# Head softmax of a two-layer hybrid: denominators over four heads instead of eight, summed by two adding transfers in a row, normalization in place

## The chip, the cores and the metric

The kernel runs on one core of a Trainium2 chip. The metric is the device time of one execution in microseconds (us); the median over runs is what is compared.

## The reference

The reference is a chain of two layers over 2 x 1024 tokens of width 128: latent attention, a spiking FFN, a state-space block, the spiking FFN again, linear attention, an FFN of eight experts, attention with 16 heads of width 8, and the experts once more. The change lies in the attention with 16 heads, whose softmax runs over the heads (axis 1), not over the keys:

```python
qkv = x @ w_qkv + b_qkv
qkv = qkv.reshape(b, n, 3, N_HEADS, HEAD_DIM)
qkv = jnp.transpose(qkv, (2, 0, 3, 1, 4))
q, k, v = (qkv[0], qkv[1], qkv[2])
dp = jnp.einsum('bhqd,bhkd->bhqk', q, k) * SCALE
attn = jax.nn.softmax(dp, axis=1)
w_avg = jnp.einsum('bhqk,bhkd->bhqd', attn, v)
```

So for each pair of a query and a key, 16 exponentials are summed and each is divided by that sum. All data are float32.

## The kernel before

All work of this stage stands in `heads_and_experts` (L928 to L1187), in one order written out by hand (`tc.manual_schedule`). It works on 128 blocks: two batches, eight tiles of 128 queries, eight tiles of 128 keys. In a block the partitions are keys and the free dimension is 16 heads x 128 queries.

A block goes through these functions: `products` (TensorE, L1025: 16 heads of scores into the one PSUM buffer `h_s`); `maxima` (VectorE, L1039: maximum over the heads); `exponentials` (VectorE subtracts the maximum into `h_e`, L1047; ScalarE takes two exponentials of eight heads each, L1050, in place); `lower` (SP issues a transfer that copies heads 0 to 7 into `h_e2`, L1056); `upper` (POOL issues an adding transfer that adds heads 8 to 15 to it, L1060); `denominators` (TensorE adds the remaining eight slices with eight multiplications by the identity into `h_pd`, L1065; a float32 multiplication stands in the profile as two records); `inverse` (VectorE reciprocal, L1070); `normalize` (POOL multiplies all 2048 columns by the reciprocal into `h_a`, two buffers, L1075); `weigh` (TensorE, values times weights, into `h_po`, L1081).

The loop at L1137 makes one step for each i from -1 to 131 and staggers the blocks. In step i TensorE's order is: `products` of block i+1, outputs of the experts (L905), the projection when a row of blocks is done (L1145), products of the experts (L879), `denominators` of block i-1, `weigh` of block i-3. VectorE's order is: `inverse` of block i-2, two multiplications for the experts (L894), `maxima` of block i+1, an addition to the residual (L914), the subtraction of block i+1. ScalarE's is: the gates of the experts (L886), the exponentials of block i+1. POOL's is: `normalize` of block i-2, then the issue of `upper` of block i. SP issues only the copy. Every engine keeps to its order, so that an instruction that waits holds up all that is behind it. `h_pd` is one PSUM buffer shared by `denominators` and the experts' outputs; `h_e` has four buffers, `h_e2` three.

Beside this run the experts of 256-token chunks (`ExpertStream`, L837): two units in each step, 32 units in a chunk. What prepares them, and the projections of the second batch (`preparation(1)`), stands in a list `side` (L1091), whose entries are begun when enough rows of blocks are `finished` and at most eight units are left; `aside(place)` puts one of their steps at its place. A step in which a preparing TensorE step is taken has no expert products (L1147). Units that are left at the end are worked off by the loop at L1179. After it `experts_ffn(g, w, [3])` works on the last 512 tokens alone.

Of the kernel before, what the change touches and what calls it, by code (L numbers as in the profile page):

```python
# [9 lines left out]
F32 = mybir.dt.float32  # L10
BF16 = mybir.dt.bfloat16
AF = mybir.ActivationFunctionType
ALU = mybir.AluOpType
# [6 lines left out]
P = 128  # L20
# [907 lines left out]
def heads_and_experts(g, w, first, second):  # L928

    nc, tc = g.nc, g.tc  # L930
    J, K, HD, H = 4, 4, 8, 16
    scale = HD**-0.5
    with ExitStack() as es:
# [3 lines left out]
        work = pool("h_work", 2)  # L937
# [20 lines left out]
        ex = ExpertStream(g, w, ework, ps_e)  # L958
# [61 lines left out]
        def spread(b):  # L1020
            v = vs[b].rearrange("p t (j k d) -> p (t j) k d", j=J, k=K)
            for k in range(K):
                nc.scalar.copy(vz[:, :, k, k, :], v[:, :, k, :])

        def products(b, qb, kb):  # L1025

            s = ps_s.tile([P, J, 512], F32, name="h_s")
            for j in range(J):
                quad = slice(32 * j, 32 * j + 32)
                nc.tensor.matmul(  # L1030
                    s[:, j, :].rearrange("p (k q) -> p k q", k=K),
                    kTs[b][quad, bass.ts(kb, P)],
                    qzs[b][quad, :, bass.ts(qb, P)],
                    start=True,
                    stop=True,
                )
            return s.rearrange("p j (k q) -> p (j k) q", k=K)

        def maxima(heads):  # L1039
            m = work.tile([P, P], F32, name="h_m")  # L1040
            nc.vector.tensor_reduce(m, heads.rearrange("p h q -> p q h"), AX.X, ALU.max)  # L1041
            return m

        def exponentials(heads, m):

            e = work.tile([P, H, P], F32, name="h_e", bufs=4)
            nc.vector.tensor_sub(e, heads, m.unsqueeze(1).to_broadcast([P, H, P]))  # L1047
            for half in range(2):
                eh = e[:, 8 * half : 8 * half + 8, :]
                nc.scalar.activation(eh, eh, AF.Exp, scale=scale)  # L1050
            return e


        def lower(e):
            e2 = work.tile([P, 8, P], F32, name="h_e2", bufs=3)
            nc.sync.dma_start(out=e2, in_=e[:, 0:8, :])  # L1056
            return e2

        def upper(e2, e):
            nc.gpsimd.dma_start(out=e2, in_=e[:, 8:16, :], accum_op=ALU.add)  # L1060

        def denominators(e2):
            pd = ps_d.tile([P, 4, D], F32, name="h_pd")[:, 0, :]
            for k in range(8):
                nc.tensor.matmul(pd, g.ident, e2[:, k, :], start=(k == 0), stop=(k == 7))  # L1065
            return pd

        def inverse(pd):
            r = work.tile([P, P], F32, name="h_r")
            nc.vector.reciprocal(r, pd)  # L1070
            return r

        def normalize(e, r):
            a = work.tile([P, H, P], F32, name="h_a")
            nc.gpsimd.tensor_mul(a, e, r.unsqueeze(1).to_broadcast([P, H, P]))  # L1075
            return a

        def weigh(kb, a, po):
            for k in range(K):
                for j in range(J):  # L1080
                    nc.tensor.matmul(  # L1081
                        po[32 * j : 32 * j + 32, :],
                        vz[:, kb * J + j, k].rearrange("p a d -> p (a d)"),
                        a[:, 4 * j + k, :],
                        start=(kb == 0 and k == 0),
                        stop=(kb == TPB - 1 and k == K - 1),
                    )

        side = [(2 * c + 2, ex.opening(c)) for c in second]  # L1091
        side.insert(2, (0, preparation(1)))
        side = [(0, ex.opening(c)) for c in first[1:]] + side
        finished, current, head = 0, None, None

        def aside(place):

            nonlocal current, head
            while True:
                if head is None:  # L1100
                    if current is None:
                        if not side or side[0][0] > finished or len(ex.units) > 8:
                            return False
                        current = side.pop(0)[1]
# [15 lines left out]
        blocks = [(b, qb, kb) for b in range(B) for qb in range(TPB) for kb in range(TPB)]  # L1120
        n = len(blocks)
        with tc.manual_schedule(engines=ALL):
            for _, step in ex.opening(first[0]):
                step()
            for place, step in preparation(0):
                step()
                if place != "act":
                    po = ps_d.tile([P, 4, D], F32, name="h_pd")
                    ex.outputs(po)
                    ex.add()  # L1130
                    ex.products()
                    ex.gates()
                    ex.multiply()
            spread(0)
            e_, e2_, d_, a_ = {}, {}, {}, {}
            oT = po = None
            for i in range(-1, n + 4):  # L1137
                if i + 1 < n:
                    heads = products(*blocks[i + 1])
                r = inverse(d_.pop(i - 2)) if 0 <= i - 2 < n else None  # L1140
                if ex.ready or oT is not None:
                    pd = ps_d.tile([P, 4, D], F32, name="h_pd")
                    ex.outputs(pd)
# [12 lines left out]
                aside("act")  # L1156
                ex.gates()
                if i + 1 < n:
                    e_[i + 1] = exponentials(heads, m)
                    e2_[i + 1] = lower(e_[i + 1])  # L1160
                aside("dve")
                if 0 <= i - 1 < n:
                    d_[i - 1] = denominators(e2_.pop(i - 1))
                if r is not None:
                    a_[i - 2] = normalize(e_.pop(i - 2), r)
                if 0 <= i < n:
                    upper(e2_[i], e_[i])
                aside("pool")
                if 0 <= i - 3 < n:
                    b, qb, kb = blocks[i - 3]  # L1170
                    if kb == 0:
                        po = ps_o.tile([P, P], F32, name="h_po")
                    weigh(kb, a_.pop(i - 3), po)
                    if kb == TPB - 1:
                        oT = work.tile([P, P], F32, name="h_oT")
                        nc.scalar.copy(oT, po)
                        if qb == TPB - 1 and b + 1 < B:
                            spread(b + 1)
            while ex.units or ex.fresh or ex.gated or ex.ready or side or current:  # L1179
                while any([aside(place) for place in ("dve", "act", "pool", "pe")]):  # L1180
                    pass
                po = ps_d.tile([P, 4, D], F32, name="h_pd")
                ex.outputs(po)
                ex.add()
                ex.products()
                ex.gates()
                ex.multiply()  # L1187
# [91 lines left out]
def kernel(ctx: ExitStack, tc: tile.TileContext, d: dict, out: bass.AP):  # L1279
# [108 lines left out]
```

## Time and profile before

| what | us |
|---|---|
| median of 3 runs (2315.94 to 2333.15) | 2323.1 |
| profiled execution, its own time | 2328.53 |
| its span, first to last instruction | 2326.8 |
| first to last `maxima` (L1041), 127 steps | 1307.8 to 2190.2 |
| last projection of the heads (L1145) | 2217.1 |
| first instruction of the last experts on TensorE (L96) | 2237.37 |

The profile is of one execution, 5.4 us above the median of the runs. From 1307.8 to 2190.2 it shows TensorE busy for 818.39 us, VectorE for 791.66, ScalarE for 612.54, POOL for 689.90, and a mean DMA share of 0.59. "Idle before" in its rows is the time for which an engine stood still just before an instruction, with the one that released it. The records of matmuls overlap, so times between starts are better than durations for TensorE.

### The profile page before, as it was taken

Reading aid. Unit: us, or ns where it says so; the run is one execution under the profiler, and the core shown is the slowest. Engines: PE = TensorE matmul, PEld = TensorE weight load, DVE = VectorE, ACT = ScalarE, POOL = GpSimd, SP = SyncE. Lnnn points to the kernel's source line nnn. Section 1 sums busy time; section 2 is a strip of 40 time slices with the busy share of each in tenths; the row PEclk is TensorE's granted clock in tenths of the full one; section 3 lists DMA queues with packets and bytes.
Section 4 is the critical chain, followed back from the end, with each engine's and each line's share of the span. In section 5 each row is a group of like instructions: output and inputs, shape, how many; then the busy total and the mean of one; then the engine's idle time right before and its main releaser. Section 6 shows DMA issues by size and latency. Waiting matters only on the chain. (4 is left out here: it accounts for less than half of the span.)

```text
span 2326.8 us, 36810 instructions
## 1 busy us (share of the span) xinstructions
PE 2015.9 (87%) x15152; PEld 1184.5 (51%) x15152; DVE 1629.0 (70%) x1988; ACT 1183.5 (51%) x1486; POOL 854.9 (37%) x460
## 2 busy tenths in 40 slices
PE   7779988887987748789698799999977999999999
PEld 4323344323334313235345577677755777777754
DVE  5851047788974659993423699899978999999732
ACT  1014521353643458764322576777735777777632
POOL 0001100033320000000102277878788787877700
PEclk9789997878998879899799899999989999999999
DMA  3000000076732067640000266566556665665500
GB/s 86 1 1 1 2 1 1 18 190 152 185 93 89 4 159 184 162 106 0 1 1 0 64 153 157 145 152 157 146 150 152 157 155 155 153 162 146 137 5 5
DMA packets 72647, 220.19 MB, mean 95 GB/s; under 512 B 9056, under 2 KB 19744, under 8 KB 72352
## 3 DMA queue, kind: packets, MB, share of 16 engines
q1 hardware_dynamic: 53584, 149.40, 21.5%
q0 software_dynamic: 18432, 67.12, 15.3%
q8 instruction: 119, 1.95, 0.3%
q10 hardware_dynamic: 464, 1.33, 0.3%
q14 instruction: 48, 0.39, 0.1%
HBM read 78.35 MB, written 5.24 MB: 36 GB/s over the span
## 5 line engine op out<-in xcount | busy, mean ns | idle before, releaser
L1075 POOL TENSOR_TENSOR h_a<-h_e,h_r 128x2048 f32<-128x2048 f32 x128 | 581.4, 4542 | 130.4 <-PE h_po L1081 93.9
L1041 DVE TENSOR_REDUCE h_m<-h_s 128x128 f32<-128x2048 f32 x128 | 293.2, 2291 | 73.2 <-PE h_s L1030 73.1
L1065 PE MATMUL h_pd<-h_e,ident 128*128 128x128 f32 x2048 | 267.4, 285 | 43.4 <-DMA h_e<-h_e 29.6
L1050 ACT ACTIVATE h_e<-h_e 128x1024 f32<-128x1024 f32 x256 | 256.5, 1049 | 89.6 <-DVE h_e L1047 71.4
L1047 DVE TENSOR_TENSOR h_e<-h_s,h_m 128x2048 f32<-128x2048 f32 x128 | 292.6, 2286 | 3.4 <-DVE h_m L1041 1.7
L1065 PEld LDWEIGHTS h_pd<-h_e,ident 128*128 128x128 f32 x2048 | 244.6, 196 | 87.3 <-DVE x_res L914 41.5
L304 POOL TENSOR_SCALAR_AFFINE_SELECT a_pT<-a_pT 128x256 f32<-128x256 f32 x128 | 97.2, 775 | 431.4 <-ACT a_pT L301 430.5
L301 ACT ACTIVATE a_pT<-a_st 128x1024 f32<-128x1024 f32 (+1 forms) x192 | 145.1, 808 | 139.1 <-PE a_st L291 137.0
L886 ACT ACT_TABLE_LOAD x105 | 134.7, 1283 | 150.5 <-PE e_pgu L879 150.3
L806 DVE TENSOR_TENSOR e_h<-e_sg,e_pu 128x512 f32<-128x512 f32 x128 | 87.0, 686 | 176.5 <-PE e_pu L802 151.2
L243 DVE TENSOR_REDUCE a_nm<-a_s 128x2 f32<-128x1024 f32 (+7 forms) x144 | 168.4, 1218 | 48.5 <-PE a_s L234 24.2
L804 ACT ACTIVATE e_sg<-e_pg 128x512 f32<-128x512 f32 x128 | 76.0, 596 | 192.5 <-PE e_pg L801 192.3
L825 PE MATMUL e_po<-e_h,Wd 128*128 128x512 f32 x256 | 139.4, 630 | 39.4 <-DVE e_h L806 39.3
L225 PE MATMUL a_s<-a_latT,a_qT 32*128 32x512 f32 (+3 forms) x768 | 128.7, 650 | 49.4 <-DVE a_nm L243 47.6
L905 PEld LDWEIGHTS h_pd<-Wd,e_h 128*128 128x128 f32 x1024 | 125.5, 191 | 90.1 <-DVE e_h L894 76.8
L1030 PE MATMUL h_s<-h_qz,h_kT 32*128 32x512 f32 x1024 | 148.5, 649 | 19.5 <-DVE h_e L1047 13.9
L879 PE MATMUL e_pgu<-e_uT,Wg 128*128 128x256 f32 x512 | 154.1, 383 | 4.0 <-ACT h_qz L994 2.1
L905 PE MATMUL h_pd<-Wd,e_h 128*128 128x128 f32 x1024 | 149.1, 287 | 5.9 <-DVE e_h L894 3.7
L879 PE MATMUL e_pgu<-e_uT,Wu 128*128 128x256 f32 x512 | 152.3, 379 | 0.0
L1060 POOL DMA_DIRECT2D h_e<-h_e x128 | 113.6, 887 | 104.0 <-DVE h_m L1041 48.8
L638 DVE TENSOR_TENSOR_SCAN s_h<-s_a,s_h 128x1024 f32<-128x1024 f32 x64 | 147.4, 2303 | 5.9 <-ACT s_a L606 1.7
L801 PE MATMUL e_pg<-e_uT,Wg 128*128 128x512 f32 x256 | 141.9, 638 | 2.1 <-ACT e_uT L794 2.1
(246 smaller groups left out, 3191.6 us busy)
## 6 DMA issues: line engine op xcount, KB each, us to landing
h_e<-h_e SPq DMA_DIRECT2D x128, 512.0 KB, 4.0
h_e<-h_e POOLq DMA_DIRECT2D x128, 512.0 KB, 4.6
s_a<-s_steps SPq DMA_DIRECT2D x64, 512.0 KB, 4.8
s_h<-s_steps SPq DMA_DIRECT2D x64, 512.0 KB, 6.3
s_steps<-s_delta SPq DMA_DIRECT2D x4, 512.0 KB, 2.6
s_steps<-s_dtx SPq DMA_DIRECT2D x4, 512.0 KB, 3.4
Wg<-in_Wg_dram SPq DMA_DIRECT2D x8, 256.0 KB, 6.0
Wu<-in_Wu_dram SPq DMA_DIRECT2D x8, 256.0 KB, 5.9
```

The costliest lines, as they stand in the source:

```text
L243: nc.vector.tensor_reduce(nm[:, half, i, h : h + together], s[:, :, :n], AX.X, ALU.max, negate=True)
L301: nc.scalar.activation(pT[:, :, off:], s[:, :, off:], AF.Exp)
L638: nc.vector.tensor_tensor_scan(h, a, h, 0.0, ALU.mult, ALU.add)
L801: nc.tensor.matmul(pg, w["Wg"][:, e, f], opened[n], start=True, stop=True)
L879: nc.tensor.matmul(pgu[:, k, :], w[name][:, e, f], uT, start=True, stop=True)
L905: nc.tensor.matmul(po[:, t, :], h[:, bass.ts(t, P)], self.w["Wd"][:, e, fc, :], start=(k == 0), stop=(k == 1))
L1030: nc.tensor.matmul(s[:, j, :].rearrange("p (k q) -> p k q", k=K), kTs[b][quad, bass.ts(kb, P)], qzs[b][quad, :, bass.ts(qb, P)], start=Tru ...
L1041: nc.vector.tensor_reduce(m, heads.rearrange("p h q -> p q h"), AX.X, ALU.max)
L1047: nc.vector.tensor_sub(e, heads, m.unsqueeze(1).to_broadcast([P, H, P]))
L1050: nc.scalar.activation(eh, eh, AF.Exp, scale=scale)
L1065: nc.tensor.matmul(pd, g.ident, e2[:, k, :], start=(k == 0), stop=(k == 7))
L1075: nc.gpsimd.tensor_mul(a, e, r.unsqueeze(1).to_broadcast([P, H, P]))
```

## The change

`h_e` gets six buffers, and `h_a` goes: the weights are normalized in place. ScalarE takes a third exponential, of heads 0 to 3, straight into `h_e2`, ahead of the two others. SP copies only heads 4 to 7, into the other half of `h_e2`. POOL's adding transfer of heads 8 to 15 stays, and a second one, `fold`, adds the upper half of `h_e2` to its lower half one step later. TensorE then sums four slices. Each of `denominators`, `inverse`, `normalize` and `weigh` comes one step later for its block; the loop is one step longer; `denominators` stand ahead of `exponentials` in the program. The preparation of the second batch stands one place earlier in `side`, and may begin with 24 units left.

```diff
         def exponentials(heads, m):
-            e = work.tile([P, H, P], F32, name="h_e", bufs=4)
+            e = work.tile([P, H, P], F32, name="h_e", bufs=6)
+            e2 = work.tile([P, 8, P], F32, name="h_e2", bufs=3)
             nc.vector.tensor_sub(e, heads, m.unsqueeze(1).to_broadcast([P, H, P]))
+            nc.scalar.activation(e2[:, 0:4, :], e[:, 0:4, :], AF.Exp, scale=scale)
             for half in range(2):
                 eh = e[:, 8 * half : 8 * half + 8, :]
                 nc.scalar.activation(eh, eh, AF.Exp, scale=scale)
-            return e
-        def lower(e):
-            e2 = work.tile([P, 8, P], F32, name="h_e2", bufs=3)
-            nc.sync.dma_start(out=e2, in_=e[:, 0:8, :])
-            return e2
+            nc.sync.dma_start(out=e2[:, 4:8, :], in_=e[:, 4:8, :])
+            return e, e2
...
+        def fold(e2):
+            nc.gpsimd.dma_start(out=e2[:, 0:4, :], in_=e2[:, 4:8, :], accum_op=ALU.add)
         def denominators(e2):
             pd = ps_d.tile([P, 4, D], F32, name="h_pd")[:, 0, :]
-            for k in range(8):
-                nc.tensor.matmul(pd, g.ident, e2[:, k, :], start=(k == 0), stop=(k == 7))
+            for k in range(4):
+                nc.tensor.matmul(pd, g.ident, e2[:, k, :], start=(k == 0), stop=(k == 3))
...
         def normalize(e, r):
-            a = work.tile([P, H, P], F32, name="h_a")
-            nc.gpsimd.tensor_mul(a, e, r.unsqueeze(1).to_broadcast([P, H, P]))
-            return a
+            nc.gpsimd.tensor_mul(e, e, r.unsqueeze(1).to_broadcast([P, H, P]))
+            return e
...
-        side = [(2 * c + 2, ex.opening(c)) for c in second]
-        side.insert(2, (0, preparation(1)))
-        side = [(0, ex.opening(c)) for c in first[1:]] + side
+        side = [(2 * c + 2, 8, ex.opening(c)) for c in second]
+        side.insert(1, (0, 24, preparation(1)))
+        side = [(0, 8, ex.opening(c)) for c in first[1:]] + side
...
-                        if not side or side[0][0] > finished or len(ex.units) > 8:
+                        if not side or side[0][0] > finished or len(ex.units) > side[0][1]:
...
-            for i in range(-1, n + 4):
+            for i in range(-1, n + 5):
                 if i + 1 < n:
                     heads = products(*blocks[i + 1])
-                r = inverse(d_.pop(i - 2)) if 0 <= i - 2 < n else None
+                r = inverse(d_.pop(i - 3)) if 0 <= i - 3 < n else None
...
+                if 0 <= i - 2 < n:
+                    d_[i - 2] = denominators(e2_.pop(i - 2))
                 if i + 1 < n:
-                    e_[i + 1] = exponentials(heads, m)
-                    e2_[i + 1] = lower(e_[i + 1])
+                    e_[i + 1], e2_[i + 1] = exponentials(heads, m)
                 aside("dve")
-                if 0 <= i - 1 < n:
-                    d_[i - 1] = denominators(e2_.pop(i - 1))
                 if r is not None:
-                    a_[i - 2] = normalize(e_.pop(i - 2), r)
+                    a_[i - 3] = normalize(e_.pop(i - 3), r)
                 if 0 <= i < n:
                     upper(e2_[i], e_[i])
+                if 0 <= i - 1 < n:
+                    fold(e2_[i - 1])
                 aside("pool")
-                if 0 <= i - 3 < n:
-                    b, qb, kb = blocks[i - 3]
+                if 0 <= i - 4 < n:
+                    b, qb, kb = blocks[i - 4]
```

More of the change, by code (lines that the diff above doesn't have):

```diff
@@ L1101, in aside @@
                     if current is None:
-                        if not side or side[0][0] > finished or len(ex.units) > 8:
+                        if not side or side[0][0] > finished or len(ex.units) > side[0][1]:
                             return False
-                        current = side.pop(0)[1]
+                        current = side.pop(0)[2]
                     head = next(current, None)
@@ L1157, in heads_and_experts @@
                 ex.gates()
+                if 0 <= i - 2 < n:
+                    d_[i - 2] = denominators(e2_.pop(i - 2))
                 if i + 1 < n:
-                    e_[i + 1] = exponentials(heads, m)
-                    e2_[i + 1] = lower(e_[i + 1])
+                    e_[i + 1], e2_[i + 1] = exponentials(heads, m)
                 aside("dve")
-                if 0 <= i - 1 < n:
-                    d_[i - 1] = denominators(e2_.pop(i - 1))
                 if r is not None:
-                    a_[i - 2] = normalize(e_.pop(i - 2), r)
+                    a_[i - 3] = normalize(e_.pop(i - 3), r)
                 if 0 <= i < n:
                     upper(e2_[i], e_[i])
+                if 0 <= i - 1 < n:
+                    fold(e2_[i - 1])
                 aside("pool")
-                if 0 <= i - 3 < n:
-                    b, qb, kb = blocks[i - 3]
+                if 0 <= i - 4 < n:
+                    b, qb, kb = blocks[i - 4]
                     if kb == 0:
                         po = ps_o.tile([P, P], F32, name="h_po")
-                    weigh(kb, a_.pop(i - 3), po)
+                    weigh(kb, a_.pop(i - 4), po)
                     if kb == TPB - 1:
```

## The prediction

> **What bounds the kernel now.** I read the costliest groups first, then the waits of this stage, then one step of the timeline, then the landings of the transfers.
>
> ```profile
> L1075 POOL TENSOR_TENSOR h_a<-h_e,h_r 128x2048 f32<-128x2048 f32 x128 | 581.4, 4542 | 130.4 <-PE h_po L1081 93.9
> L1065 PE MATMUL h_pd<-h_e,ident 128*128 128x128 f32 x2048 | 267.4, 285 | 43.4 <-DMA h_e<-h_e 29.6
> ```
>
> The sums by the identity are the largest TensorE group of the stage, and POOL's normalization is long but has 130 us of idle time before it. The waits say who holds whom:
>
> ```profile
> POOL h_a L1075 <- PE h_po L1081: 93.9, 86, 2.7
> DVE h_m L1041 <- PE h_s L1030: 73.1, 114, 2.2
> POOL h_e L1060 <- DMA h_e<-h_e: 37.6, 29, 2.8
> PE h_pd L1065 <- DMA h_e<-h_e: 29.6, 28, 3.4
> ```
>
> VectorE and POOL wait for TensorE, which waits only now and then for a transfer. One step shows it:
>
> ```profile
> 1606.43 2.28 DVE L1047 TENSOR_TENSOR h_e<-h_s,h_m 128x2048 f32<-128x2048 f32 x1
> 1606.57 2.05 PE L1065 MATMUL h_pd<-h_e,ident 128*128 128x128 f32 x16
> 1607.41 0.86 POOL L1060 DMA_DIRECT2D h_e<-h_e  x1
> 1608.55 1.08 PE L1081 MATMUL h_po<-h_a,h_vz 128*32 128x128 f32 x32
> 1608.66 0.96 DVE L1070 RECIPROCAL h_r<-h_pd 128x128 f32<-128x128 f32 x1
> 1609.13 2.00 ACT L1050 ACTIVATE h_e<-h_e 128x1024 f32<-128x1024 f32 x2
> 1609.53 0.69 DVE L894 TENSOR_TENSOR e_h<-e_sg,e_pgu 128x256 f32<-128x256 f32 x2
> 1609.56 1.14 PE L1030 MATMUL h_s<-h_qz,h_kT 32*128 32x512 f32 x8
> 1609.81 4.52 POOL L1075 TENSOR_TENSOR h_a<-h_e,h_r 128x2048 f32<-128x2048 f32 x1 [1.53 <-PE h_po L1081]
> 1610.77 2.29 DVE L1041 TENSOR_REDUCE h_m<-h_s 128x128 f32<-128x2048 f32 x1 [0.55 <-PE h_s L1030]
> ```
>
> From start to start TensorE needs 1.07 (scores), 1.08 (L905), 1.73 (L879), 1.98 (L1065), 1.02 us (L1081): with the waits between, 6.87 us, the commonest distance of two `maxima`. From the first to the last it is 882.4 us / 127 = 6.948. VectorE has only 0.55 us free; its starts add up to 0.87 + 0.62 + 2.21 + 0.33 + 2.23 = 6.26.
>
> ```profile
> L1060 POOL DMA_DIRECT2D h_e<-h_e x128: 840/876/1190, 1317.2 to 2200.6; - x128
> DMA to landing us min/median/max: 4.5/4.6/6.0
> L1056 SPq DMA_DIRECT2D h_e<-h_e x128: 464/465/528, 1313.6 to 2196.5; - x128
> DMA to landing us min/median/max: 2.9/4.0/5.9
> ```
>
> By the packets' own records the adding transfer issued at 1607.41 has its first packet at 1608.85, its last ends at 1611.62, it lands at 1611.99: 1.45 + 2.77 + 0.36. The copy issued at 1610.21 runs from 1611.43 to 1612.87: 1.22 + 1.44 + 0.36. A copy that comes while an adding transfer runs does not mix with it: issued at 1746.03, its first packet is at 1748.34, as the adding one ends (1748.53). And a waiting POOL issues late: in all 29 waits, 0.56 us after the last landing (1621.89 to 1622.45).
>
> **The change, part by part.**
>
> TensorE loses 8 of 16 records of L1065 in a step, 1.98/2 = 0.99 us: its step falls to about 5.9. That alone would hand the step to VectorE, 6.26.
>
> ScalarE gains an exponential of 512 columns. Nearest row: the expert gate of 512 columns, 596 ns; I take 0.6. Its step is 1.28 + 0.66 + 1.28 + 0.6 + 2.0 = 5.8, hidden; but SP's copy is issued 0.6 later, and behind this exponential are the two others, the copy, and so `upper`. It also waits for the `denominators` three blocks back (three buffers of `h_e2`): nothing while they end (1614.7) ahead of the subtraction (1615.8), the excess when `fold` lands over a microsecond late.
>
> POOL gains an issue of 0.86 in a step: 4.47 + 0.86 + 0.86 = 6.2, and the wait for L1081 (93.9 us) goes with `h_a`. So POOL, too, could follow a step of 6.3. Thirteen side steps on POOL, 1.6 us each, have some 0.8 us cover: +5 us (0 to 10).
>
> Transfers: the copy halves, 1.44 to 0.72 us of packets. `fold` is not in the trace. Its rows are half as long as those of `upper`: 1.4 us of packets if time goes by bytes, 2.77 if it goes by rows. Copied rows take 0.159 us for 4 KB, added ones 0.341, as if by bytes read; I take 1.42. `fold` is issued 0.86 after `upper` of the next block, on the same queue, so its packets follow: landing 1.45 + 2.77 + 1.42 + 0.36 = 6.0 us after the issue of `upper`.
>
> Two chains come of it. **Chain one**, three steps long: landing of `fold`, 0.13 to the first matmul (seen in 28 waits), sums 1.0, `weigh` 1.02, scores to `maxima` 1.2, on to the reciprocal 2.21 + 0.33 + 2.23 = 4.77, reciprocal 0.96, 0.18 to POOL, normalization 4.47: 13.73, then 6.0 to the next landing. 19.73 / 3 = 6.58 us a step. **Chain two**, one step: `upper` waits for its block's copy; if that copy's packets come after those of `fold`: 1.45 + 2.77 + 1.42 + 0.72 + 0.36 + 0.56 = 7.28. If the copy goes between the two, chain two is 5.86, but `fold` lands 0.72 later and chain one is 20.45 / 3 = 6.82.
>
> Which? The Trainium skill, "DMA: Bandwidth & Descriptors", Queues, rings and completion order, says that an engine changes between queues only after a whole packet group. The trace agrees (no mixing), so the copy goes between if it is there when `upper` ends, so if issued within 4.22 - 1.22 = 3.0 us of `upper`. At 6.82 us a step chain one puts the copy's issue 13.73 + 6.72 - 0.96 - 0.18 - 4.47 + 0.12 + 1.68 = 16.6 us after the `upper` of two steps before, so 16.6 - 13.64 = 3.0 after its own: on the edge. I take the middle, 7.05: (7.05 - 6.948) x 127 = +13 us.
>
> A rule that speaks for the change stands on the same page, Anatomy of one DMA: a POOL transfer costs about 2.0 us + bytes/436 GB/s, 3.2 us for 512 KB. The row has 4.6. By the rule both packet runs are 1.8 us, `fold` lands after 3.6, chain one is 17.3 / 3 = 5.8 and VectorE bounds at 6.3: about 70 us faster. I go by the row.
>
> Chance delays: in this stage the instruction queue fetches 63 packets, about 1 us each on one of the 16 engines. Before, TensorE's bound hid most (mean less mode is 0.08 x 127 = 10 us). Now the transfers are in both chains without slack: an estimate of half of 63 at 0.65 us, +20 (0 to 40).
>
> The side list: counting through it, steps without expert products fall from 26 of 133 to 22 of 134. At two units a step that leaves 10 of 224 units before (with four in flight, seven rounds) and none after. From the last projection (2217.1) to the last experts (2237.37) go 20.3 us; what remains is their opening, seen at 2217.9 to 2223.9 beside those rounds, some 7: -13 (0 to -15).
>
> Drain: the last block passes `fold` alone: 0.56 + 1.45 + 1.42 + 0.36 less 1.0 of matmuls = 2.8, at most one step, 7: +5.
>
> Sum: 13 + 5 + 20 - 13 + 5 = +30: the profiled execution from 2328.5 to 2358, the median from 2323.1 to **2353**.
>
> **Rivals.**
> The transfers keep up (**faster**): if `fold` lands within 3 x 6.3 - 13.73 = 5.2 us of `upper`'s issue instead of 6.0, because its packets overlap the end of `upper`'s, VectorE bounds; with some waits 6.45: -63 - 13 + 5 = -71, 2252. For it: no row shows two adding transfers back to back. Against: 2.77 + 1.42 us of packets are needed anyhow.
> The copy always gets between, and the fetches are absorbed (**no change**): 6.89, -7 - 13 + 5 + 5 = 2313.
> It never does: 7.28 and 0.1 of delays, +55 + 10 + 5 - 13 + 5: 2385. For it: the 0.6 us by which the copy is later. If `fold` goes by rows, chain two is 8.6 and the time is past 2500; the rows of the copy speak against it.
>
> **Numbers.** Mine 0.40, faster 0.12, no change 0.22, never between 0.26. Runs of this kernel tell about 1% from no change, so the bounds are 2300 and 2346. Faster: its rival and a sliver of the second, 0.13; the rest of that and the low end of mine, 0.25; slower 0.62. The range for 8 in 10 leaves out the fast rival and the slowest tail: 2298 to 2396; mine alone has 2335 to 2370.
>
> **What would show it.** 1024 records of L1065; idle time before L1075 no longer for L1081; `upper` waiting for the copy in far more than 29 steps, and L1065 for `fold`; a `fold` landing 5 to 6 us after its own issue; VectorE idle over 0.55 us a step. Wrong: steps of 6.3 to 6.4 with VectorE without gaps, or landings of `fold` under 4 us.

## The result, and the profile after

The changed kernel takes 2394.18 us (median of 4 runs, 2387.01 to 2397.62) beside 2322.2 us for the one before (4 runs, 2315.94 to 2333.15): a ratio of 1.0301, 95% interval 1.0270 to 1.0331, **slower by 3%**. The forecast was 2353: the sign was right, and the loss of 72 us is 2.4 times the +30 of its sum. The time lies 2 us inside the upper end of the forecast's range (2298 to 2396) and 9 us above the 2385 of its rival "It never does". The profiled execution took 2397.62 us, its span is 2395.9.

The page of the changed kernel has these lines: the chain that ended last (section 4), the groups that answer to those shown of before (section 5: busy us, mean ns, then idle time before and its releaser) and the transfers (section 6: KB each, median us from issue to landing).

```profile
PE 28%; DVE 14%; DMA 13%; issue 7%; ACT 6%; POOL 3%; SPq 0%; POOLq 0%; DVEq 0%; ACTq 0%
...
L1076 POOL TENSOR_TENSOR h_e<-h_e,h_r 128x2048 f32<-128x2048 f32 x128 | 623.2, 4869 | 34.3 <-DVE h_r L1072 34.3
...
L1067 PE MATMUL h_pd<-h_e,ident 128*128 128x128 f32 x1024 | 156.5, 300 | 169.5 <-DMA h_e<-h_e 74.7
...
L1059 POOL DMA_DIRECT2D h_e<-h_e x128 | 117.2, 916 | 172.7 <-DMA h_e<-h_e 88.9
...
L1062 POOL DMA_DIRECT2D h_e<-h_e x128 | 155.3, 1213 | 0.5 <-issue 0.5
...
h_e<-h_e POOLq DMA_DIRECT2D x128, 512.0 KB, 4.6
...
h_e<-h_e SPq DMA_DIRECT2D x128, 256.0 KB, 3.8
h_e<-h_e POOLq DMA_DIRECT2D x128, 256.0 KB, 5.9
```

The page's chain that ended last can be followed over 71% of the span, and transfers are 13%. (On the page of before it is 3% of a chain that covers only 24%, so the two shares are not to be compared.) The sums have half their records (1024 of L1067), and TensorE now stands idle for 169.5 us before them, the largest part of it, 74.7, for a transfer, where it was 43.4. `fold` (the 256 KB row of POOL's queue) lands 5.9 us after its own issue, inside the 5 to 6 us that the forecast named. The waits of the stage name the same two landings; the columns are us in total, times, longest:

```profile
ACT L1050 <- DVE h_e L1049: 114.5, 84, 2.4
POOL h_e L1059 <- DMA h_e<-h_e: 88.9, 74, 2.8
PE h_pd L1067 <- DMA h_e<-h_e: 74.7, 46, 3.8
DVE h_m L1041 <- PE h_s L1030: 81.8, 105, 2.9
```

`upper` (L1059) stands waiting for its copy 74 times where it was 29; by the starts and landings of the trace it is issued 0.56 us after that landing in some 114 of 127 steps (the table puts part of the waits down to other releasers). The first line is one that the forecast had not: ScalarE's first exponential now starts with its table load only after the subtraction. It had to be tried as a cause of its own.

One step of the changed kernel's timeline:

```profile
1839.56 1.08 PE L1082 MATMUL h_po<-h_e,h_vz 128*32 128x128 f32 x32
1839.61 0.87 POOL L1059 DMA_DIRECT2D h_e<-h_e  x1 [1.31 <-DMA h_e<-h_e]
...
1840.19 1.18 POOL L1062 DMA_DIRECT2D h_e<-h_e  x1
...
1840.78 5.15 POOL L1076 TENSOR_TENSOR h_e<-h_e,h_r 128x2048 f32<-128x2048 f32 x1
...
1841.78 2.29 DVE L1041 TENSOR_REDUCE h_m<-h_s 128x128 f32<-128x2048 f32 x1 [0.48 <-PE h_s L1030]
1842.33 0.47 SPq L1054 DMA_DIRECT2D h_e<-h_e  x1
...
1846.24 1.13 PE L1067 MATMUL h_pd<-h_e,ident 128*128 128x128 f32 x8 [1.71 <-DMA h_e<-h_e]
1846.67 1.28 ACT L1050 ACT_TABLE_LOAD   x1 [1.45 <-DVE h_e L1049]
1846.87 0.87 POOL L1059 DMA_DIRECT2D h_e<-h_e  x1 [0.94 <-DMA h_e<-h_e]
```

`upper` is issued at 1839.61, `fold` 0.58 later, the copy of the next block at 1842.33, 2.72 after `upper`. By the packets' own records `upper` runs from 1841.05 to 1843.86, then `fold` from 1843.72 to 1845.68 and the copy from 1844.11 to 1845.88, mixed. They land at 1844.21, 1846.11 and 1846.31. TensorE's sums start 0.13 after the landing of `fold`, the next `upper` 0.56 after that of the copy, 7.26 us after its predecessor. The forecast's chain two, with the copy behind `fold`, was 7.28.

**Where the +69.1 us of span are.** From first to last `maxima` the stage takes 963.2 us instead of 882.4, 7.585 us a step instead of 6.948: +80.8. From the last `maxima` to the last projection it is 37.2 instead of 26.9 (+10.3), from there to the last experts 3.2 instead of 20.3 (-17.1), the last experts themselves take 4.6 longer, and the first `maxima` came 9.5 earlier (what stands ahead of it is the same code; in the sixteen profiles it takes from 1294.5 to 1307.8).

Steps also divide by the instruction fetches: in the stage of the changed kernel 61 packets of 16 KB, about 1.1 us each on one of the 16 engines, and 27 of 8 KB. The 54 steps that have none between two `upper` take 7.33 us in the mean and 7.28 in the middle; the 59 with one 7.77 and 7.61, the 14 with more 8.06. What a fetch does to a single transfer can be seen too: 29 `upper` transfers had a fetch running while their packets ran (1.45 to 4.2 us after the issue), and these landed after 5.59 us in the middle, the 99 others after 4.60. What it costs a step is less sure: counted between two `maxima`, steps with a fetch and without take 7.58 and 7.59.

### The profile page after: what moved, and what is told of

Read it like the earlier page. It is cut to its first block, busy times and chain, and to the rows that moved or that the text cites. A ratio compares the mean times of both kernels' runs of the same rounds, so it can differ in the third digit from the quotient of the medians.

```text
span 2395.9 us, 35203 instructions
## 1 busy us (share of the span) xinstructions
PE 1936.4 (81%) x14128; PEld 1089.5 (45%) x14128; DVE 1629.3 (68%) x1988; ACT 1278.3 (53%) x1623; POOL 974.0 (41%) x588
## 4 chain that ended last, share of the span: by engine, by line
PE 28%; DVE 14%; DMA 13%; issue 7%; ACT 6%; POOL 3%; SPq 0%; POOLq 0%; DVEq 0%; ACTq 0%
DMA h_e<-h_e 13%; DVE h_e L1049 4%; PE e_pg L801 4%; PE e_po L825 3%; PE e_pu L802 3%; PE h_pd L1067 3%; PE h_s L1030 3%; PE e_pgu L879 2%; PE h_po L1082 2%; DVE s_h L638 2%; ACT h_e L1053 2%; PE h_pd L905 2%; ACT L1050 1%; POOL h_e L1076 1%; PE s_pm L487 1%
## 5 line engine op out<-in xcount | busy, mean ns | idle before, releaser
L1076 POOL TENSOR_TENSOR h_e<-h_e,h_r 128x2048 f32<-128x2048 f32 x128 | 623.2, 4869 | 34.3 <-DVE h_r L1072 34.3
L1067 PE MATMUL h_pd<-h_e,ident 128*128 128x128 f32 x1024 | 156.5, 300 | 169.5 <-DMA h_e<-h_e 74.7
L1067 PEld LDWEIGHTS h_pd<-h_e,ident 128*128 128x128 f32 x1024 | 135.7, 205 | 214.0 <-issue 145.0
L1050 ACT ACT_TABLE_LOAD x110 | 141.1, 1283 | 131.5 <-DVE h_e L1049 114.5
L1059 POOL DMA_DIRECT2D h_e<-h_e x128 | 117.2, 916 | 172.7 <-DMA h_e<-h_e 88.9
L1030 PE MATMUL h_s<-h_qz,h_kT 32*128 32x512 f32 x1024 | 161.0, 701 | 23.8 <-DVE h_e L1049 18.6
L1072 DVE RECIPROCAL h_r<-h_pd 128x128 f32<-128x128 f32 x128 | 122.1, 954 | 83.7 <-PE h_pd L1067 83.3
L225 PE MATMUL a_s<-a_latT,a_qT 32*128 32x512 f32 (+3 forms) x768 | 118.9, 592 | 53.6 <-DVE a_nm L243 51.8
L879 PE MATMUL e_pgu<-e_uT,Wg 128*128 128x256 f32 x512 | 156.7, 388 | 2.6 <-ACT h_qz L994 2.1
L1062 POOL DMA_DIRECT2D h_e<-h_e x128 | 155.3, 1213 | 0.5 <-issue 0.5
L1082 PE MATMUL h_po<-h_e,h_vz 128*32 128x128 f32 x4096 | 154.9, 298 | 0.0
```

The costliest lines, as they stand in the source:

```text
L879: nc.tensor.matmul(pgu[:, k, :], w[name][:, e, f], uT, start=True, stop=True)
L1030: nc.tensor.matmul(s[:, j, :].rearrange("p (k q) -> p k q", k=K), kTs[b][quad, bass.ts(kb, P)], qzs[b][quad, :, bass.ts(qb, P)], start=Tru ...
L1050: nc.scalar.activation(e2[:, 0:4, :], e[:, 0:4, :], AF.Exp, scale=scale)
L1076: nc.gpsimd.tensor_mul(e, e, r.unsqueeze(1).to_broadcast([P, H, P]))
L1082: nc.tensor.matmul(po[32 * j : 32 * j + 32, :], vz[:, kb * J + j, k].rearrange("p a d -> p (a d)"), a[:, 4 * j + k, :], start=(kb == 0 and ...
```

## The experiments

Three theories stood at the start. (A) The transfers: the copy comes behind `fold` and holds the next `upper`, or `fold` lands late and holds the sums. (B) ScalarE: the exposed table load and the third exponential make everything behind them late. (C) POOL: its second issue makes its step too long. Some runs fell outside all the ranges expected for them; where this bears on the argument, it is said. Steps below are mean distances of two `maxima`; "clean" is the mean distance of two `upper` without a fetch between them, where it is used.

| run | median us | ratio to before, 95% | step us |
|---|---|---|---|
| e1, `fold` ahead of `upper` | 2342.94 | 1.0069 (1.0052 to 1.0087) | 7.145 |
| e2, table load early | 2399.47 | 1.0303 (1.0254 to 1.0353) | 7.613 |
| e3, no copy | 2337.18 | 1.0047 (1.0032 to 1.0062) | 7.149 |
| e4, no `fold` | 2318.06 | 0.9969 (0.9952 to 0.9985) | 6.965 |
| e5, before with the new side list | 2320.26 | 0.9975 (0.9961 to 0.9990) | 7.026 |
| e6, before normalized in place | 2331.12 | 1.0022 (1.0008 to 1.0036) | 7.001 |
| e7, e1 and e3 | 2307.29 | 0.9914 (0.9877 to 0.9951) | 6.835 |
| e8, half of `fold` | 2334.29 | 1.0040 (1.0024 to 1.0056) | 7.071 |
| e9, rows' copy on VectorE | 2390.78 | 1.0283 (1.0244 to 1.0322) | 7.482 |
| e10, e7 and e9 | 2279.58 | 0.9811 (0.9776 to 0.9846) | 6.663 |
| e11, e4 and e9 | 2311.04 | 0.9940 (0.9922 to 0.9957) | 6.929 |
| e12, e10, other order of exponentials | 2281.43 | 0.9817 (0.9781 to 0.9852) | 6.674 |
| e13, copy issued early | 2399.44 | 1.0327 (1.0281 to 1.0372) | 7.607 |
| e14, e3 and e9 | 2325.20 | 0.9994 (0.9974 to 1.0014) | 7.051 |

### e1: the fold ahead of the other adding transfer

```diff
-                if 0 <= i < n:
-                    upper(e2_[i], e_[i])
                 if 0 <= i - 1 < n:
                     fold(e2_[i - 1])
+                if 0 <= i < n:
+                    upper(e2_[i], e_[i])
```

> Only POOL's order changes: in each step the fold of the last block is issued ahead of the upper transfer of the next one. Theory A (the queue of transfers sets the step: upper, then fold, then the copy, then the next upper, 7.26 us in an undisturbed step): the fold no longer stands between upper and copy, the step falls to 6.4 to 6.7 us and the time to 2270 to 2300. Theory B (the exponentials' table load that now stands behind the subtraction, and so a later copy, sets it): the copy is no earlier, the time stays within 2370 to 2400. Theory C (POOL's own work, a second issue of 1.2 us and longer normalizations, sets it): POOL has the same instructions, no change, 2385 to 2400.

Measured: 2342.94 us, a step of 7.145: less gain than (A) expected, more than (B) and (C) allow. POOL issues the same instructions as in the changed kernel, and 51 us are gone, so (C) falls as the cause of the loss; it comes back in e10. The waits of e1 and the transfers of its page show what took the place of the old wait:

```profile
PE h_pd L1067 <- DMA h_e<-h_e: 97.3, 76, 3.7
...
POOL h_e L1062 <- DMA h_e<-h_e: 73.4, 86, 4.1
```

```profile
h_e<-h_e POOLq DMA_DIRECT2D x128, 512.0 KB, 6.1
h_e<-h_e SPq DMA_DIRECT2D x128, 256.0 KB, 3.5
h_e<-h_e POOLq DMA_DIRECT2D x128, 256.0 KB, 3.4
```

`fold` lands 3.4 us after its issue instead of 5.9, but `upper`, whose packets now follow, needs 6.1 instead of 4.6, and the next `fold` (L1062) stands waiting for that landing. The wait has moved to the other adding transfer of the same queue, at a lower price.

### e2: the table load ahead of the exponentials

```diff
+        hot = one.tile([P, 1], F32, name="h_hot")
...
             nc.vector.tensor_sub(e, heads, m.unsqueeze(1).to_broadcast([P, H, P]))
+            nc.scalar.activation(hot, g.eps, AF.Exp)
```

> One tiny exponential of a constant column is put ahead of the three of a block, so that the table load runs before the subtraction has ended; the exponentials start some 1.2 us earlier. Theory A: the copy comes earlier in the queue, but upper and fold are as before; a part of the delay goes, 2330 to 2370. Theory B: the step falls by about 0.9 us, 2270 to 2300. Theory C: no change, 2385 to 2400.

Measured: 2399.47 us, 1.0303; the step is 7.613. The small exponential no longer waits for the subtraction, and the table load goes with it. The copy is issued 2.33 us after `upper` in the middle instead of 3.03, and the step is no shorter. Of the waits of e2:

```profile
ACT h_e L1052 <- PE h_pd L1069: 105.2, 92, 5.8
```

ScalarE's third exponential, which writes into `h_e2`, now stands waiting for the `denominators` three blocks back (L1069), the wait that the forecast named. So the 114.5 us in the profile were spare time in front of a chain that closes elsewhere, and (B) falls.

### e3: without the copy

```diff
-            nc.scalar.activation(e2[:, 0:4, :], e[:, 0:4, :], AF.Exp, scale=scale)
+            nc.scalar.activation(e2, e[:, 0:8, :], AF.Exp, scale=scale)
...
-            nc.sync.dma_start(out=e2[:, 4:8, :], in_=e[:, 4:8, :])
```

> ScalarE writes the exponentials of all eight lower heads straight into the sum's buffer (0.4 us more for it), and SP's copy is gone; upper waits for ScalarE only. Theory A: the chain upper, fold, copy, upper is cut, what is left is the path of a block over three steps, about 6.6 us: 2280 to 2310. Theory B: the table load still stands behind the subtraction, little change, 2370 to 2400. Theory C: no change, 2385 to 2400.

Measured: 2337.18 us, a step of 7.149, again less gain than (A) expected. ScalarE does more work than in the changed kernel, and 57 us are gone with the copy. These 57 and the 51 of e1 are not to be added: both edits together (e7) bring 87. The page of e3 has a new holder of the chain that ended last, POOL with 31% of the span, and transfers with 1%.

### e4 and e8: no fold, and half of it

e4:

```diff
-                if 0 <= i - 1 < n:
-                    fold(e2_[i - 1])
...
-            for k in range(4):
-                nc.tensor.matmul(pd, g.ident, e2[:, k, :], start=(k == 0), stop=(k == 3))
+            for k in range(8):
+                nc.tensor.matmul(pd, g.ident, e2[:, k, :], start=(k == 0), stop=(k == 7))
```

> The fold is left out and TensorE sums eight slices again; everything else of the change stays (in place, one step later, the third exponential, half a copy, the side list). Theory A: without the fold's packets the queue has 5.8 us a step, TensorE sets the step again, 6.87 us: 2300 to 2325. Theory B: the table load stays, 2360 to 2390. Theory C: POOL is relieved of one issue, 2310 to 2340.

e8:

```diff
-            nc.gpsimd.dma_start(out=e2[:, 0:4, :], in_=e2[:, 4:8, :], accum_op=ALU.add)
+            nc.gpsimd.dma_start(out=e2[:, 4:6, :], in_=e2[:, 6:8, :], accum_op=ALU.add)
...
-            for k in range(4):
-                nc.tensor.matmul(pd, g.ident, e2[:, k, :], start=(k == 0), stop=(k == 3))
+            for k in range(6):
+                nc.tensor.matmul(pd, g.ident, e2[:, k, :], start=(k == 0), stop=(k == 5))
```

> The fold adds two heads instead of four (rows of 1 KB instead of 2), TensorE sums six slices instead of four; order and copy as in the change. Theory A by bytes: its packets take 0.7 us instead of 1.4, the step falls from 7.58 by about 0.7 to 6.9, 2305 to 2330. If it is the fixed part of a transfer (issue, first packet, landing, wait) and not its packets: the step stays within 0.2 us, 2370 to 2400.

Measured: without `fold` 0.9969 and a step of 6.965, that of before again; with half its bytes 1.0040 and 7.071. So `fold` with the four fewer sums is the whole loss; the split exponentials, the halved copy and the normalization in place, which e4 keeps beside the side list, cost nothing that can be told. In e8 a row of 1 KB takes 0.105 us in the middle where one of 2 KB took 0.181; with eight rows for each of the 16 engines that is 0.61 us of packets less, and the step is 7.585 - 7.071 = 0.51 us shorter, though TensorE has two more sums. The waits of e4 show `upper` free again:

```profile
POOL h_e L1059 <- DMA h_e<-h_e: 20.5, 17, 2.8
```

### e5 and e6: the side list alone, in place alone

Both are the kernel before with one part of the change. e5:

```diff
-        side = [(2 * c + 2, ex.opening(c)) for c in second]
-        side.insert(2, (0, preparation(1)))
-        side = [(0, ex.opening(c)) for c in first[1:]] + side
+        side = [(2 * c + 2, 8, ex.opening(c)) for c in second]
+        side.insert(1, (0, 24, preparation(1)))
+        side = [(0, 8, ex.opening(c)) for c in first[1:]] + side
...
-                        if not side or side[0][0] > finished or len(ex.units) > 8:
+                        if not side or side[0][0] > finished or len(ex.units) > side[0][1]:
...
-                        current = side.pop(0)[1]
+                        current = side.pop(0)[2]
```

> The kernel before, with the new side list alone. Theory A (the prediction's term for the list): no units are left at the end of the loop, the stretch from the last projection to the last experts falls from 20 to about 4 us, steps stay at 6.9 us: 2305 to 2312. Rival: the list's gain is given back in the steps that now carry the units, 2318 to 2328.

e6:

```diff
-            e = work.tile([P, H, P], F32, name="h_e", bufs=4)
+            e = work.tile([P, H, P], F32, name="h_e", bufs=6)
...
-            a = work.tile([P, H, P], F32, name="h_a")
-            nc.gpsimd.tensor_mul(a, e, r.unsqueeze(1).to_broadcast([P, H, P]))
-            return a
+            nc.gpsimd.tensor_mul(e, e, r.unsqueeze(1).to_broadcast([P, H, P]))
+            return e
```

> The kernel before, with normalization in place and six exponential buffers, nothing else. POOL no longer waits for the weighing two blocks back. Theory A: TensorE sets the step, 6.87 us, so nothing is gained: 2315 to 2328. Rival (POOL's wait was part of what set the step): 2290 to 2310.

Measured: e5 0.9975. From the last projection to the last experts it takes 3.2 us instead of 20.3, but the step is 7.026, (7.026 - 6.948) x 127 = 10 us more, the way from the last `maxima` to the last projection 2.8 longer, and the last experts take 4.4 longer. In this profile that gives back all of the 17; in the medians some 6 are left. The rival had it right. e6 1.0022, no gain but a loss of some 5 us. Its waits say why there is no gain:

```profile
POOL h_e L1074 <- DVE h_r L1070: 116.9, 110, 3.8
```

POOL's 93.9 us of waiting for `weigh` are gone, and POOL waits for the reciprocal instead, which waits for TensorE's sums: the wait was not what held the step. What makes it slower was not looked for.

### e7: the fold first and no copy

Both edits, that of e1 and that of e3.

> The change with the fold issued ahead of upper and without SP's copy (ScalarE writes eight heads). Theory A: fold's packets start without a queue before them, upper waits for no copy; the chain left in the queue is fold, upper, landing, next fold, 1.45 + 1.42 + 2.77 + 0.36 + 0.3 = 6.3 us, about VectorE's 6.26: steps of 6.4 to 6.7, 2260 to 2300. Rival: something else of the change (three exponentials with the table load behind the subtraction, one step more) holds the step near 7.1: 2325 to 2345.

Measured: 2307.29 us, 0.9914, below the kernel before and between the two expected ranges. The middle step is 6.317, the mean 6.835, so a few steps are long. The timeline of e7 at the end of a row of eight blocks:

```profile
1829.33 1.04 ACT L1053 ACTIVATE h_e<-h_e 128x1024 f32<-128x1024 f32 x1
1830.28 0.25 ACT L1177 COPY h_oT<-h_po 128x128 f32<-128x128 f32 x1
...
1830.58 0.80 PE L1145 MATMUL h_pd<-w_proj,h_oT 128*128 128x128 f32 x2 [3.58 <-ACT h_oT L1177]
...
1831.16 1.06 PE L879 MATMUL e_pgu<-e_uT,Wg 128*128 128x256 f32 x2
```

A copy of 0.25 us (L1177, the weighted values of a row for the projection) stands on ScalarE behind the exponentials; TensorE waits 3.58 us for it, once in eight steps. The steps in which a row's projection falls take 9.88 us in the mean in e7. In the changed kernel they take 7.90 beside a mean of 7.585; there the wait is mostly hidden (14.9 us in all, 12 times). The matmuls after the wait then take 1.06 us a pair instead of 0.59.

### e9, e10, e11: the rows' copy on VectorE

```diff
-                        nc.scalar.copy(oT, po)
+                        nc.vector.tensor_copy(oT, po)
```

> The change, but VectorE instead of ScalarE copies the finished row of blocks (h_oT) out of PSUM, once in eight steps. In e7 TensorE's projection waited some 3 us a row for that copy, which stands behind the exponentials on ScalarE. Theory A (in the change itself the queue of transfers sets the step, and the late copy is mostly hidden under it; its wait in the profile is 15 us in all): 2375 to 2392. Rival (the late copy costs the change as much as e7, 16 x 3.4 = 54 us): 2335 to 2350.

> Fold ahead of upper, no copy by SP, and h_oT copied by VectorE. Theory A: every step is then VectorE's, 6.3 us; from e7's 2307 go 16 x 3.4 = 54 us less 16 x 0.3 for the copy on VectorE: 2250 to 2275. Rival (another wait takes the place of the row's): 2285 to 2305.

> The change without the fold (eight slices summed by TensorE, as in e4) and with h_oT copied by VectorE: what the rest of the change brings when neither the queue nor the row's copy is in the way. TensorE sets the step, 6.75 us: from e4's 2318 go 16 x 1.4 = 22 us: 2290 to 2302. Rival (the row's wait is hidden): 2312 to 2320.

Measured: the same edit is worth 3 us on the changed kernel (e9, less than the runs tell), 7 without `fold` (e11), and 28 by the medians, 24 by the ratios, where the transfers no longer bound (e10). For e10 and e11 this is less than the expectations had. e10 is the **best version: 2279.58 us, 1.9% below the kernel before**, with the changed kernel's four sums. Of its page the chain that ended last, POOL's normalization and the transfers, and its windows row (stretch; then us busy and number of instructions of PE, PEld, DVE, ACT, POOL; granted TensorE clock, DMA share, GB/s):

```profile
POOL 32%; PE 20%; DVE 10%; issue 3%; ACT 3%; DMA 3%; POOLq 0%; SPq 0%; DVEq 0%; ACTq 0%
...
L1075 POOL TENSOR_TENSOR h_e<-h_e,h_r 128x2048 f32<-128x2048 f32 x128 | 666.9, 5210 | 4.6 <-DVE h_r L1071 4.6
...
h_e<-h_e POOLq DMA_DIRECT2D x128, 512.0 KB, 5.5
h_e<-h_e POOLq DMA_DIRECT2D x128, 256.0 KB, 3.3
```

```profile
1310.00:2140.00 830.00, 729.40 (x7596) 521.02 (x7596) 778.50 (x770) 742.59 (x833) 794.29 (x394) 0.97 0.65 119
```

VectorE is busy for 778.50 of 830 us (94%), and `maxima` wait for the scores for 33.0 us in all instead of 81.8. But POOL is fuller still, 794.29 us (96%): the last chain stands on POOL for 32% of the span, and its normalization has 4.6 us of idle time before it where it was 130.4 before and 34.3 in the changed kernel. Where POOL does not wait, its two issues and its normalization follow one another, from end to end, after 0.90, 0.89 and 4.58 us in the middle: 6.37 us, and the middle of the clean steps is 6.38 (the mean of all 6.663). VectorE's starts add up to 6.26. So theory (C), wrong for the changed kernel, is what the page shows for the best version; as no run relieves POOL alone, that is read from the trace and not shown by an experiment. The forecast's fast rival had 6.45 and VectorE for the cause: near in number, but not for that reason.

### e12: another order of the exponentials

```diff
+            nc.scalar.activation(e[:, 8:16, :], e[:, 8:16, :], AF.Exp, scale=scale)
             nc.scalar.activation(e2, e[:, 0:8, :], AF.Exp, scale=scale)
-            for half in range(2):
-                eh = e[:, 8 * half : 8 * half + 8, :]
-                nc.scalar.activation(eh, eh, AF.Exp, scale=scale)
+            nc.scalar.activation(e[:, 0:8, :], e[:, 0:8, :], AF.Exp, scale=scale)
```

> As e10, with the exponentials of heads 8 to 15 ahead of the others, so that the table load and the first of them no longer stand behind the wait for the denominators. If VectorE sets the step, no difference to e10 beyond 0.5%. If ScalarE's late start still does: 10 to 25 us less than e10.

Measured: 2281.43 us, 0.9817, not to be told from e10. When ScalarE's exponentials begin no longer sets the step.

### e13: the copy issued early

```diff
-            nc.scalar.activation(e2[:, 0:4, :], e[:, 0:4, :], AF.Exp, scale=scale)
-            for half in range(2):
-                eh = e[:, 8 * half : 8 * half + 8, :]
-                nc.scalar.activation(eh, eh, AF.Exp, scale=scale)
+            nc.scalar.activation(e[:, 4:8, :], e[:, 4:8, :], AF.Exp, scale=scale)
             nc.sync.dma_start(out=e2[:, 4:8, :], in_=e[:, 4:8, :])
+            nc.scalar.activation(e[:, 8:16, :], e[:, 8:16, :], AF.Exp, scale=scale)
+            nc.scalar.activation(e2[:, 0:4, :], e[:, 0:4, :], AF.Exp, scale=scale)
+            nc.scalar.activation(e[:, 0:4, :], e[:, 0:4, :], AF.Exp, scale=scale)
```

> The change with ScalarE's exponentials split so that heads 4 to 7 come first, then 8 to 15, then 0 to 3 twice: SP's copy is issued some 2 us earlier, within about 1 us of upper's issue instead of 3.0; transfers, sums and POOL's order are as in the change. In the profile of the change the two steps whose copy came within 2 us of upper had the next upper 5.85 us later. Theory A (upper, fold, copy, next upper): the copy is always ahead of the fold, its wait is gone, and the path of a block over three steps is left, 6.8 us and delays of 0.3: 2395 less about 0.5 x 127, so 2325 to 2345. Rival (the late fold alone sets the step, the copy's place does not matter): 2380 to 2400.

Measured: 2399.44 us, no gain. As a test of "copy ahead of `fold`" it is inconclusive: the copy came earlier, at 2.1 us after `upper` in the middle, and that was not early enough. (It follows the end of its exponential by 0.03 us in 116 of 125 steps, so it is ScalarE's order and not a buffer of `h_e2` that holds it.) Its single steps show where the edge lies; all times are from the issue of `upper`, in the middle. All 13 copies issued up to 1.08 us went ahead of `fold`: the copy lands at 5.26, `fold` at 6.72, and the next `upper` follows after 6.14. Of the 42 issued between 1.13 and 2.0 us 3 went ahead; in these steps the two mix as before (copy 6.73, `fold` 6.55), and the next `upper` follows after 7.30. In the changed kernel the 57 steps with the copy at 2.0 to 3.0 us mix as well (copy 6.8, `fold` 6.55).

### e14: what the place of the fold costs by itself

The edits of e3 and e9: e10 with `fold` back behind `upper`, e9 without the copy.

> The changed kernel without SP's copy (ScalarE writes all eight heads of the second buffer itself) and with the rows' copy of the weighted values on VectorE, the fold still behind the adding transfer of the next block. Between this run and the changed kernel with only the rows' copy moved (step 7.48) lies the copy alone; between this run and the best version so far (step 6.66) lies only the place of the fold. Theory that the chain of three steps now bounds (6.58 worked out for a copy that is not between): undisturbed steps of 6.6 to 6.8, a mean of 6.85 to 6.95 with the fetches, 2290 to 2310 us. Theory that with the copy gone nothing of the fold's place matters and VectorE bounds: mean 6.65, 2280 us. Theory that the place of the copy is not what counted: mean above 7.2, over 2340 us.

Measured: 2325.20 us, 0.9994, above the 2290 to 2310 that were expected. The clean steps, 6.77 us, lie where the chain of three steps put them; the mean is 7.051, with more lost to the rest than I had allowed. `fold` lands 6.14 us after `upper`'s issue. That the chain of three steps is what bounds here is not shown, though: the page of e14 has POOL with 31% of the span in the chain that ended last and transfers with 2%, much as that of e3. The way from the changed kernel to the best one is, by the steps of the profiles: rows' copy 7.585 - 7.482 = 0.10 us a step, the transfer's copy 7.482 - 7.051 = 0.43, the place of `fold` 7.051 - 6.663 = 0.39. Over 127 steps the last two are 55 and 49 us. The profile of e9 is of the fastest of its four runs, 9 us under their median; by the ratios of the medians the two are 67 and 43 us. Both count; which counts for more, these runs tell only roughly.

## Why the prediction was right or wrong

**Right: what the transfers cost, and what bounded before.** 1.42 us of packets for `fold`, by bytes: a record of 2 KB took 0.178 us, one of 4 KB 0.341. Chain two with the copy behind was worked out as 7.28; the clean steps have 7.28 in the middle. `fold` after `upper`'s issue: 6.0 forecast, 6.14 in e14. Chain one without a copy between was worked out as 6.58, and the clean steps of e14 have 6.77; as the chain on its page stands on POOL, that nearness may be luck. Without `fold` (e4) the step is TensorE's 6.965 again, as the reading of before had it. And the row was the better guide than the rule of the Trainium skill, "DMA: Bandwidth & Descriptors", Anatomy of one DMA, whose estimate for the 512 KB transfer was 3.2 us: it landed after 4.6 in the changed kernel too, and the 70 us of gain that the rule led to did not come.

**Wrong: the step "so the copy goes between if it is there when `upper` ends", and with it "on the edge. I take the middle, 7.05".** The place of the copy was worked out well, 3.0 us after `upper`; the middle of 126 steps is 3.03. What failed is the edge: put at 3.0 us, it lies at 1.1 in e13. In all but two steps of the changed kernel the copy was late, so the step is the 7.28 of chain two, which the forecast had left to its rival "It never does", and not something between 6.82 and 7.28. The forecast gave the copy its turn when `upper` ends, at 4.2 us, and left out that `fold` stands in line by then: issued 0.58 us after `upper`, its packets are due at 0.58 + 1.45 = 2.03, while the copy needs 1.22 from its issue and would have to start by 0.8 to be due first. (With the forecast's 0.86 for 0.58 it is 1.1.) That the one due first goes first is an estimate that comes near the edge seen; no run tests it by itself. The row of before that showed "no mixing" had only one adding transfer in POOL's queue and could not answer this. Taken at clean steps (mean 7.33) the term is (7.33 - 6.948) x 127 = +49 us instead of +13.

**Too small: the chance delays.** Forecast +20, from 63 fetches; the stage of before has 68 of 16 KB and 23 of 8 KB. The mean step lies 7.585 - 7.33 = 0.25 us above the clean ones, +32. Steps with a fetch between two `upper` are longer by 0.3 to 0.8 us in fifteen of the sixteen traces, the one of before included; in e3 they are not. A transfer that meets a fetch lands later, by 1.0 us (5.59 beside 4.60), but no run took the fetches away, so how much of the +32 they cause is not shown. The half "hidden" that I assumed had little to hide in: in the changed kernel the copy's landing releases `upper` in some 114 of 127 steps.

**The ends of the stage and the side list.** The drain was 10.3 us instead of 5; in e10, without the copy, it is 5.7. The side list gave 17.1 at its place instead of 13, but the forecast put its cost in the steps and in the last experts at nothing: alone (e5) the list is worth some 6 us in the median. POOL's side steps (+5) are inside the steps and can't be told apart. The sum of forecast terms was 13 + 5 + 20 - 13 + 5 = 30; measured it is 49 + 32 + 10.3 - 17.1 = 74, and with -9.5 ahead of the stage and 4.6 behind it some 69. The split into 49 and 32 hangs on how clean steps are counted; their sum, 80.8 for the steps where the forecast had 38, does not. The rival "It never does" came to 2385; its chain two is what ran, though one term of its sum, +10, has no name.

**ScalarE and POOL.** ScalarE's third exponential was costed as hidden, and is; that its table load would come to stand behind the subtraction I did not see, and e2 shows that it costs nothing while the transfers bound. POOL was costed as able to follow a step of 6.3, and in e10 it is the fullest engine, at a step of 6.38 in the middle of the clean steps.

**What stays open.** Why `fold`, behind `upper` on one queue, starts no later than a copy that has waited on another since before `upper` ended (its packets were due at 1843.55 in the step shown, and `fold`'s first came at 1843.72, the copy's at 1844.11) is not explained by any run. The rule of the Trainium skill on whole packet groups ("DMA: Bandwidth & Descriptors", Queues, rings and completion order), as the forecast read it, does not fit the mixed steps: a copy has 128 rows and 16 closing packets of 4 bytes, and in the step shown the first closing packet comes 1.6 us after the first row, where it is 0.67 in copies that meet no adding row. So the rows of the two transfers alternate, and the measurement decides. And a copy that is ahead of `fold` in all steps was not reached, so the price of a late `fold` with a copy between was not measured.

## What to carry to other kernels

Before sums go from a busy engine to a second transfer, add up the packets of all transfers of a step and follow each landing to who waits for it: here 2.8 + 1.4 + 0.7 us of packets with 1.8 us of start and landing and 0.6 of waking are longer than TensorE's step was. Which transfer goes first matters as much as its time: `fold` first and the copy replaced by ScalarE's own writing turned +3.0% into -0.9%. When a bound is gone, look for short instructions that stand behind long ones in an engine's order: 0.25 us of copy were then worth 24 to 28 us. And add up the next engine in line as carefully: here it was POOL, which the change had given a second issue.

## What the runs showed that I had not expected

A waiting TensorE was granted less clock. The windows rows of the stage have 0.98 before, 0.94 in the changed kernel, 0.96 in e7 and, shown above, 0.97 in e10, in the order of how long TensorE stands idle. After the wait of 3.58 us in e7 pairs of L879 took 1.06 us instead of 0.59, and from 1830.0 to 1836.7 the granted clock was 0.50, after 1.00 up to 1829.9. The rows of before, the changed kernel and e7:

```profile
1307.80:2190.20 882.40, 818.39 (x8629) 623.87 (x8629) 791.66 (x755) 612.54 (x717) 689.90 (x275) 0.98 0.59 151
```

```profile
1310.00:2250.00 940.00, 751.84 (x7548) 538.65 (x7548) 778.55 (x749) 693.44 (x843) 790.79 (x392) 0.94 0.67 140
```

```profile
1310.00:2170.00 860.00, 743.29 (x7617) 533.98 (x7618) 782.35 (x763) 753.87 (x854) 798.47 (x396) 0.96 0.64 116
```

Records of POOL overlap, so that durations mislead. The second transfer's issue reads as 1.18 us instead of 0.87, and the normalization behind it as 4.87 in the mean instead of 4.54. Both records begin while the instruction before still runs (1840.19 against 1839.61 + 0.87, and 1840.78 against 1840.19 + 1.18 in the step shown). Counted from the end of the instruction before it, the second issue takes 0.89 us and the normalization 4.56 in the middle, so neither is really longer.
